# Pools that end with their stage, Toeplitz terms on four row groups, and a new order in the expert stage

## The chip, the cores and the metric

The kernel runs on one core of a Trainium2 chip. The core has five engines that work from queues of their own, each in order: TensorE (PE, with its weight loads listed as PEld), VectorE (DVE), ScalarE (ACT), GpSimd (POOL) and SyncE (SP), which here issues the DMAs. The metric is device microseconds of one execution, the median of several runs. All data are 32-bit floats.

## The reference

Four stages run one after another on x of shape 16 x 256 x 128; each result is added to its input and normalised.

```python
x = ln(x + attn_rel(x))      # 16 heads of 8; logits q.k + q.a_k + k.a_q + a_q.a_k,
                             # a_* = E*[clip(l - m, -64, 64) + 64]; out = attn.v + attn.a_v
x = ln(x + local(x))         # 6 layers: 16 heads of 64, window 32, look-back attention with
                             # rotary terms, then norm, W1 (gelu gate), W2; 64 channels shifted
x = ln(x + causal(x))        # causal attention, 16 heads of 8
x = ln(x + moe(x))           # 8 experts of 64, top 2 of softmax(x @ gate_w)
# moe
gates = softmax(xt @ gate_w);  topk_g, topk_i = top_k(gates, 2)
tok_w = topk_g.sum(-1);        sel = one_hot(topk_i).any(1)
h = gelu(einsum('nd,edh->enh', xt, w1) + b1)
y = einsum('enh,ehd->end', h, w2) + b2
out = einsum('end,ne,n->nd', y, sel, tok_w)
```

## The kernel before

The activations stay in on-chip memory from the first stage to the last, as 16 batches of two tiles of 128 rows (`xb`, and `xa` from the second stage on). PSUM is shared out once for the whole program: `big()` hands out one of 2 buffers of 128 x 1024 (two banks each), `small()` one of 4 buffers of 128 x 512 (one bank each). A stage opens its own pools of on-chip memory when it starts and closes them when it ends; pools lie one behind the other, so the pools of the next stage lie over those of the last. What a new tile waits for is set by the pools that it lies over: all tiles of such a pool must be done with.

Each stage writes out its own order: a list of steps, run again and again for a shifted batch or unit, and at the end `in_order` ties the instructions of each engine to that order. Between stages the planner follows the order of the program, but puts an instruction of a later stage into a hole of an engine when its inputs and its memory are free.

**Relative attention** (`relative_attention`, the first 815 us). One batch is eight turns (`TURNS`), each with one unit of four heads: `weights` (on PE eight transposes at L505 and four matmuls of 32 rows at L517 into a `big`; on DVE four additions with the `rq` terms, L527), `exponentials` (ACT, L543) and `turn_weights` (eight transposes at L562 into two `small`). The terms that depend on position are made once per batch. `diagonal` (128 small matmul passes, L388) makes a skewed copy `spots` of a projection. `chunk` multiplies 32 rows of it by a window of a Toeplitz table, eight matmuls at L413 into one `big`, which lie on two of the four 32-row groups of the array; `rq_chunk` takes them out by two ACT copies (L449), `rk_chunk` by two DVE additions (L470). Four chunks make `rq`, four make `rk`, so a batch has eight. `corners` (L434) makes the far corners. The results go to three sets of tiles, `terms(0..2)`: set 0 for the first half of the rows of every batch, 1 and 2 in turn for the second. All of these, with tables and masks, lie in one pool, `r_one`.

**Local attention and feed-forward** (`local_layers`, 815 to 3741 us). The list `STEPS` runs over 32 tiles of each of 6 layers with up to nine tiles in flight. Its pools (`w_cst`, `a_inp`, `a_one`, `a_two`, `a_thr`, `a_fou`) hold the buffers of the attention and of the feed-forward steps (`f_*`, `a_vo`, `a_g`) together. It begins with `fetch` (the shifted copies `a_xt`, L992 to L994), the weights (L165) and the rotary tables, all issued by SP, then `inputs` (transposes, L1029) and `project` (L1090).

**Causal attention** (`causal_attention`, 3741 to 4115 us) has eight turns per batch again. For batch 0 the steps `join`, `norm`, `scaled`, `turn`, `project_v` and `project` come ahead of the first `weights` (L1534). **Experts** (`experts`, from 4115 us) works on 8 groups of 4 tiles. `turn` makes `xT`, `score` the logits of the gates, `choose` (12 steps on DVE and one on POOL, L1791 to L1808) picks the two best experts of 16 tiles, `first` is the first product with gelu (four matmuls at L1819), `turn_gates` and `weigh` spread the chosen weights over the hidden rows and multiply (L1833, L1835, L1844, L1846), `second` is the second product (L1855, L1862) with the residual addition and the statistics on DVE (L1865 to L1874), `finish` the normalisation on ACT (L1886) and the store.

Of the kernel before, what the change touches and what calls it, by code (L numbers as in the profile page):

```python
# [242 lines left out]
def relative_attention(tc, I, xb, env):  # L243
# [21 lines left out]
    with ExitStack() as ctx:  # L265
        one = ctx.enter_context(tc.tile_pool(name="r_one", bufs=1))
# [6 lines left out]
        def terms(k):  # L273
            rq3[k] = one.tile([P, H, 2, P], F32, name=f"r_rq{k}")
            rk3[k] = one.tile([P, H, P], F32, name=f"r_rk{k}")
            rkc3[k] = one.tile([P, H, P], F32, name=f"r_rkc{k}")

        terms(1)
# [12 lines left out]
        terms(0)  # L291
# [9 lines left out]
        terms(2)  # L301
# [101 lines left out]
        def chunk(table, d, c):  # L403

            ps = big()
            for g in range(4):
                for x in range(2):
                    at = 8 * c + 4 * x + g
                    s_ = at // 16
                    r = rows_of(s_, at // 4 % 4)  # L410
                    o = C0 - 4 * at
                    rows = slice(32 * r, 32 * r + 32)
                    T.matmul(  # L413
                        ps[:, 512 * x + 128 * g : 512 * x + 128 * g + 128],
                        lhsT=table[rows, o : o + P],
                        rhs=d[rows].rearrange("p h t s g i -> p (h t) s g i")[:, :, s_, g, :],
                        start=True,
                        stop=True,
                    )
            return ps  # L420
# [24 lines left out]
        def rq_chunk(b, c):  # L445
            ps = chunk(tq, st[b]["d", "k"], c).rearrange("p (g h t i) -> p t g h i", g=8, t=NT, i=4)
            for t in range(NT):
                o = of(rq3, b, t)[:, :, 0, 32 * c : 32 * c + 32]
                A.copy(o.rearrange("p h (g i) -> p g h i", i=4), ps[:, t])  # L449
# [15 lines left out]
        def rk_chunk(b, c):  # L465
            ps = chunk(tk, st[b]["d", "q"], c).rearrange("p (g h t i) -> p t g h i", g=8, t=NT, i=4)
            pc = pp[:, 32 * c : 32 * c + 32].rearrange("p (g i) -> p g i", i=4).unsqueeze(2)
            for t in range(NT):
                o = of(rk3, b, t)[:, :, 32 * c : 32 * c + 32]
                V.tensor_add(  # L470
                    o.rearrange("p h (g i) -> p g h i", i=4), ps[:, t], bcast(pc, (P, 8, H, 4))
                )
# [186 lines left out]
        def normalise(b, lc):  # L659
# [11 lines left out]
                (1, values, 0),  # L671
                (0, rk_corners, 1),
                (-1, turn),
                (0, rk_chunk, 1),
                (2, turn_weights),
                (0, rk_chunk, 0),
                (0, rk_corners, 0),
                (-1, project),
                (1, exponentials),
                (-1, diagonal, "k"),  # L680
                (0, weights),
            ),
            (
                (2, turn_weights),
# [4 lines left out]
                (0, weights),  # L689
                (1, positions, 1),  # L690
                (2, turn_weights),
                (1, join, 0),
                (1, exponentials),
            ),
            (
                (1, exponentials),
                (0, weights),
                (-1, rq_chunk, 1),
                (1, values, 1),
                (2, turn_weights),  # L700
                (-1, rq_corners, 1),
                (-1, rq_chunk, 2),
            ),
            (
                (1, exponentials),
                (1, join, 1),
                (0, weights),
                (-1, rq_chunk, 0),
                (2, turn_weights),
                (-1, spread_k, 0),  # L710
            ),
            (
                (2, turn_weights),
                (1, exponentials),
                (1, statistics, 1),
                (0, weights),
            ),
            (
                (-1, rq_chunk, 3),
                (0, positions, 0),  # L720
                (1, normalise, 1),
                (-1, rq_corners, 0),
                (1, exponentials),
                (-1, diagonal, "q"),
                (0, weights),
                (-1, rk_chunk, 3),
                (2, turn_weights),
                (0, project_v),
                (1, statistics, 0),
            ),  # L730
            (
                (1, exponentials),
                (2, turn_weights),
                (0, weights),
                (1, normalise, 0),
                (-1, spread_k, 1),
                (-1, rk_chunk, 2),
# [157 lines left out]
def local_layers(tc, I, xa, xb, env):  # L895
# [14 lines left out]
    with ExitStack() as octx:  # L910
# [4 lines left out]
        b2 = cst.tile([P, DEPTH, D], F32, name="w_b2")  # L915
        lng = cst.tile([P, DEPTH], F32, name="w_lng")
        lnb = cst.tile([P, DEPTH], F32, name="w_lnb")
        b1 = cst.tile([P, DEPTH, 2, 3], F32, name="w_b1")
# [31 lines left out]
        fou = octx.enter_context(tc.tile_pool(name="a_fou", bufs=4))  # L950

# [86 lines left out]
        def fold(m):  # L1038
# [7 lines left out]
            if part == 0:  # L1046
# [7 lines left out]
                w["vT"], w["vo"] = wvT, two.tile([P, NP, 2, D], F32, name="a_vo")  # L1054
# [150 lines left out]
        def gather(m):  # L1205
# [16 lines left out]
            g = two.tile([P, H, P], F32, name="a_g")  # L1222
# [13 lines left out]
        def output(m):  # L1236
# [14 lines left out]
            if t == NT - 1:  # L1251
                ffn[i, b] = {"x": shifted(xa[b], fou, "f_xt")}
# [12 lines left out]
        def f_stats(i, g):  # L1265
            f = ffn[i, 2 * g]
            tiles = [ffn[i, 2 * g + k // NT]["x"][:, k % NT, :] for k in range(2 * NT)]
            mv = two.tile([P, 2 * NT, 2], F32, name="f_mv")
            for k, x in enumerate(tiles):
                s6 = two.tile([P, 6], F32, name="f_st")  # L1270
                V.bn_stats(s6, x)
                V.bn_aggr(mv[:, k], s6)
            ve = two.tile([P, 2 * NT], F32, name="f_ve")
# [3 lines left out]
        def f_power(i, g):  # L1277
            f = ffn[i, 2 * g]
            rs = two.tile([P, 2 * NT], F32, name="f_rs")
# [10 lines left out]
        def f_turn(i, g):  # L1290
# [4 lines left out]
            xn = two.tile([P, W], F32, name="f_xn")  # L1295
# [3 lines left out]
        def f_gate(i, g):  # L1299
            f, w = ffn[i, 2 * g], weights[i]  # L1300
            hT = one.tile([P, 3, W], F32, name="f_hT")
# [44 lines left out]
        def f_sum(i, g):  # L1346
# [3 lines left out]
            for k in range(2):  # L1350
                xw = two.tile([P, NT, D], F32, name="f_xw")
# [62 lines left out]
def causal_attention(tc, I, xa, xb, env):  # L1414
# [12 lines left out]
    with ExitStack() as ctx:  # L1427
# [12 lines left out]

        def join(b):
# [26 lines left out]
        def turn(b):  # L1468
            ps = small()
# [6 lines left out]
        def project(b):  # L1476

            ps = small()
# [18 lines left out]
        def project_v(b):  # L1497
            ps = small()
# [200 lines left out]
        for at in range(-NU, N + NU):  # L1699
            for behind, step, *args in TURNS[at % NU]:  # L1700
# [3 lines left out]
                elif 0 <= at // NU - behind < NB:  # L1704
                    step(at // NU - behind, *args)
        env.in_order(first)


def experts(tc, I, xa, out, env):
# [13 lines left out]
    with ExitStack() as ctx:  # L1723
# [3 lines left out]
        glp = ctx.enter_context(tc.tile_pool(name="e_glp", bufs=NH + 1))  # L1727
# [28 lines left out]
        def turn(g):  # L1756
# [4 lines left out]
            if g % 2:  # L1761
# [87 lines left out]
        def second(g):  # L1849
            hT, wT = st[g]["hT"], st[g]["wT"]  # L1850
            po = small()
# [11 lines left out]
            y = two.tile([P, NK, D], F32, name="e_y")  # L1863
            for j in range(2):
                V.tensor_add(  # L1865
                    y[:, NT * j : NT * (j + 1)],
                    po[:, j * S : (j + 1) * S].rearrange("p (t f) -> p t f", t=NT),
                    xa[2 * g + j],
                )
            mv = two.tile([P, NK, 2], F32, name="e_mv")  # L1870
            for k in range(NK):
# [3 lines left out]
            rs = two.tile([P, NK], F32, name="e_rs")  # L1875
            G.tensor_scalar_add(rs, mv[:, :, 1], LN_EPS)
            env.inv_sqrt(rs, rs)
            nm = two.tile([P, NK], F32, name="e_nm")
            G.tensor_mul(nm, mv[:, :, 0], rs)
            G.tensor_scalar_mul(nm, nm, -1.0)  # L1880
            st[g].update(y=y, rs=rs, nm=nm)

# [74 lines left out]
```

## Time and profile before

| what | us |
|---|---|
| median of 3 runs | 4238.94 (4238.55 to 8422.65) |
| the profiled execution | 4239.75 |
| its span, first to last instruction | 4237.9 |
| relative attention, to the last PE instruction | 815.2 |
| local layers, to the last PE instruction of the feed-forward | 3740.7 |
| causal attention, to its last DVE instruction | 4115.7 |
| last instruction of the expert stage | 4237.7 |

The third of the three runs, 8422.65, took twice as long as the other two, which lie 0.4 us apart; the median is one of those two. The page gives busy shares by engine, then the span in 40 slices, the DMA queues, and the chain of work that ended last, followed back from the last instruction. The trace behind it can be asked for one engine's instructions in order of time: such a row has the start, the length of a run of equal instructions, engine and line, tile written and tiles read, shape, count, and in brackets the idle time before it and what ended that. A matmul of 32-bit floats counts twice (two passes), a transpose once.

### The profile page before, as it was taken

The page shows a single profiled execution, that of the slowest core. Times are in us where ns is not written, and L with a number is a line of the kernel's source. Part 1 is how long each engine was busy: PE and PEld are TensorE (multiplying, and loading weights), DVE is VectorE, ACT ScalarE, POOL GpSimd, SP SyncE. Part 2 cuts the span into 40 slices and gives each one's busy share as a digit, 9 for nine tenths or more (in the row PEclk, how much of TensorE's full clock was granted, in tenths as well). Part 3 has the DMA queues.
Part 4 walks back from the last instruction along what each step waited for, and adds up shares of the span by engine and source line. Part 5 has one row for each costly group of instructions (what it writes and reads, how often), then busy time and mean ns, then how long its engine had stood idle before and what let it go on. Part 6 is the DMA issues. An engine that isn't in the chain of part 4 may idle for free.

```text
span 4237.9 us, 149104 instructions
## 1 busy us (share of the span) xinstructions
PE 4110.5 (97%) x62028; PEld 3021.4 (71%) x62028; DVE 3324.1 (78%) x6347; ACT 3301.8 (78%) x11368; POOL 2701.8 (64%) x3176
## 2 busy tenths in 40 slices
PE   8999999899999999999999999999999999989998
PEld 6888888666776677676776777667776677656665
DVE  5655665588888888888888888888888888769974
ACT  3666666578888888888888888888888888869973
POOL 2121211288888888888888888888888888723221
PEclk9999999999999999999999999999999999989999
DMA  1000000110000000000000000000000000000000
GB/s 36 3 3 3 3 3 3 43 30 15 19 20 24 20 21 19 25 18 17 19 20 24 20 20 19 24 18 18 19 15 24 15 14 15 9 2 2 2 8 20
DMA packets 158799, 69.51 MB, mean 16 GB/s; under 512 B 123549, under 2 KB 154276, under 8 KB 158124
## 3 DMA queue, kind: packets, MB, share of 16 engines
q1 hardware_dynamic: 158124, 59.99, 5.6%
q8 instruction: 488, 8.00, 0.8%
q14 instruction: 187, 1.53, 0.1%
HBM read 21.72 MB, written 2.12 MB: 6 GB/s over the span
## 4 chain that ended last, share of the span: by engine, by line
PE 87%; POOL 6%; ACT 3%; issue 2%; DVE 2%; DMA 0%; SPq 0%; POOLq 0%; ACTq 0%; DVEq 0%
PE small L1240 15%; PE big L1090 12%; PE small L1147 8%; PE big L1215 7%; PE big L1162 5%; PE small L1337 3%; PE small L1321 3%; PE big L505 3%; PE small L1578 3%; PE small L562 3%; PE small L1305 3%; PE big L1534 3%; POOL a_u L1129 3%; PE big L517 3%; PE big L413 2%
## 5 line engine op out<-in xcount | busy, mean ns | idle before, releaser
L1183 ACT ACTIVATE a_pr<-a_pr,a_nb 128x64 f32<-128x64 f32 x3072 | 1029.0, 342 | 5.7 <-DVE a_nb L1176 5.7
L1111 POOL TENSOR_TENSOR a_u<-a_u,a_r 128x1024 f32<-128x1024 f32 x384 | 901.2, 2369 | 28.3 <-DVE a_r L1106 23.7
L1129 POOL TENSOR_TENSOR a_u<-a_u,a_y 128x1024 f32<-128x1024 f32 x384 | 722.9, 1904 | 15.1
L1240 PE MATMUL small<-a_vo,a_g 128*128 128x128 f32 x6144 | 717.6, 275 | 1.6 <-ACT a_g L1233 1.6
L1240 PEld LDWEIGHTS small<-a_vo,a_g 128*128 128x128 f32 x6144 | 701.2, 192 | 2.6 <-ACT a_g L1233 2.5
L1101 ACT ACTIVATE a_sq<-big 128x1024 f32<-128x1024 f32 x384 | 392.0, 1022 | 268.9 <-PE big L1090 268.6
L1183 ACT ACTIVATION_READ_ACCUMULATOR a_pr<-a_pr,a_nb 128x1 f32 x3072 | 600.4, 195 | 0.0
L1147 PEld LDWEIGHTS small<-ident,a_u 128*128 128x128 f32 x3072 | 349.5, 141 | 139.9 <-POOL a_u L1129 86.8
L1118 DVE TENSOR_REDUCE a_ss<-a_sq 128x16 f32<-128x1024 f32 x384 | 446.3, 1204 | 0.0
L1147 PE MATMUL small<-ident,a_u 128*128 128x128 f32 x3072 | 401.2, 274 | 23.2 <-POOL a_u L1129 21.1
L1090 PE MATMUL big<-w_k,a_xs 128*128 128x512 f32 x768 | 387.0, 627 | 3.5 <-issue 1.6
L1195 POOL TENSOR_TENSOR a_pr<-a_pr,a_rd 128x1024 f32<-128x1024 f32 x192 | 365.8, 1905 | 13.0 <-DVE a_rd L1194 13.0
L1090 PE MATMUL big<-w_q,a_xs 128*128 128x512 f32 x768 | 362.4, 594 | 0.0
L1162 PEld LDWEIGHTS big<-a_kT,a_qT 64*32 64x32 f32 x24576 | 262.2, 105 | 126.2 <-issue 68.1
L1170 DVE TENSOR_TENSOR a_pr<-big,w_band 128x1024 f32<-128x1024 f32 x192 | 235.2, 1225 | 109.8 <-PE big L1162 109.8
L527 DVE CUSTOM_DVE_ANT_0 r_lg<-big,r_rq 128x256 f32<-128x256 f32 x512 | 186.8, 421 | 155.5 <-PE big L517 67.5
L1102 DVE TENSOR_TENSOR a_u<-big,a_tak 128x1024 f32<-128x1024 f32 x192 | 235.2, 1225 | 90.5 <-ACT a_sq L1101 90.5
L1162 PE MATMUL big<-a_kT,a_qT 64*32 64x64 f32 x24576 | 294.7, 226 | 8.7 <-POOL a_kT L1140 6.2
L1223 ACT COPY a_g<-big 128x1024 f32<-128x1024 f32 x192 | 193.8, 1009 | 105.6 <-PE small L1215 105.1
L1560 ACT ACTIVATE c_lg<-c_lg,c_nb 128x256 f32<-128x256 f32 x512 | 256.8, 520 | 4.7 <-DVE c_nb L1544 4.6
L1090 PEld LDWEIGHTS big<-w_q,a_xs 128*128 128x128 f32 x768 | 143.5, 192 | 164.0 <-issue 128.4
L543 ACT ACTIVATE r_lg<-r_lg,r_nb 128x256 f32<-128x256 f32 x512 | 254.9, 507 | 4.4 <-DVE r_nb L527 4.4
(276 smaller groups left out, 9382.6 us busy)
## 6 DMA issues: line engine op xcount, KB each, us to landing
a_xm<-a_xt SPq DMA_DIRECT2D x96, 96.0 KB
f_xt<-xa SPq DMA_DIRECT2D x96, 64.0 KB
f_xt<-xa SPq DMA_DIRECT2D x96, 63.5 KB
a_xt<-xa SPq DMA_DIRECT2D x80, 64.0 KB
a_xt<-xa SPq DMA_DIRECT2D x80, 63.5 KB
w_k<-in_L_ffn_Wqkv_dram SPq DMA_DIRECT2D x6, 512.0 KB
w_q<-in_L_ffn_Wqkv_dram SPq DMA_DIRECT2D x6, 512.0 KB
w_v<-in_L_ffn_Wqkv_dram SPq DMA_DIRECT2D x6, 512.0 KB
```

The lines of the kernel that those rows point to most:

```text
L1090: T.matmul(ps[:, c * 512 : (c + 1) * 512], lhsT=xs_of[i, b][:, t, 0:P], rhs=weights[i]["qk"[j]][:, c * 512 : (c + 1) * 512], start=True, s ...
L1101: A.activation(sq, ps3, AF.Square)
L1111: G.tensor_add(u, u, r)
L1118: V.tensor_reduce(ss[:, j], st[m]["sq", j], AX.X, ALU.add)
L1129: G.tensor_mul(u, u, bcast(y[:, j].unsqueeze(2), (P, H, DH)))
L1147: T.transpose(ps[:, k, :], u[:, o : o + P], ident)
L1162: T.matmul(ps[q0 : q0 + WIN, e, c, :], lhsT=qT[DH * e : DH * (e + 1), c, q0 : q0 + WIN], rhs=kT[DH * e : DH * (e + 1), c, t * P + q0 : t * ...
L1183: A.activation(s_["pr"][:, h], s_["pr"][:, h], AF.Exp, bias=s_["nb"][:, h : h + 1], accum_out=s_["den"][:, h : h + 1],)
L1195: G.tensor_mul(s_["pr"], s_["pr"], bcast(rd.unsqueeze(2), (P, H, DH)))
L1215: T.matmul(ps[win], lhsT=x[r, t, :], rhs=pT[r, :, o, :], start=(o == 0), stop=(o == 1),)
L1240: T.matmul(ps[:, 0:D], lhsT=st[m]["g"][:, h, :], rhs=weights[i]["vo"][:, h // 2, h % 2, :], start=(h == 0), stop=(h == H - 1),)
L1560: A.activation(lg[:, j], lg[:, j], AF.Exp, bias=nb[:, j : j + 1], scale=-1.0, accum_out=st[b, lc]["den"][:, h : h + 1],)
```

## The change

Four edits are made together.

1. In `relative_attention` the pool `r_one` is split in three. The set `terms(1)`, `spots`, the tables and the projections' weights are in `r_fst`, `terms(0)` is in `r_snd`, the rest is in `r_one`. In `local_layers` the feed-forward buffers, `a_vo`, `a_g` and four small constants go from the front and middle pools to `f_cst`, `f_one`, `f_two` and `f_fou`, which lie behind the pools of the attention.
2. `chunk` becomes `diagonals`: 16 matmuls in a row on all four row groups, into one `big` and two `small`. A batch has four such halves in place of eight chunks. A half is taken out by two operations of 128 x 512 and four of 128 x 256. The eight turns are written anew.
3. In `causal_attention` the turns up to the second unit are given high priority with the planner; the PSUM buffers of `turn`, `project` and `project_v` are a `big` for batch 0.
4. In `experts` both `choose` follow their `score`, ahead of any `first`; `first` runs three groups ahead; `weigh` of the next group stands ahead of `second` of this one; and the last group is closed in two halves, normalised on DVE.

```diff
-        one = ctx.enter_context(tc.tile_pool(name="r_one", bufs=1))
-        terms(1)
+        one = ctx.enter_context(tc.tile_pool(name="r_fst", bufs=1))
+        terms(one, 1)
         spots = one.tile([P, H, NT, 2, 4, 4], F32, name="r_d")
...
-        terms(0)
+        terms(ctx.enter_context(tc.tile_pool(name="r_snd", bufs=1)), 0)
+        one = ctx.enter_context(tc.tile_pool(name="r_one", bufs=1))
...
-        terms(2)
+        terms(one, 2)
...
-        def chunk(table, d, c):
-            ps = big()
+        def diagonals(table, d, s_):
+            both = big()
+            ps = [both[:, 0:512], both[:, 512:1024], small(), small()]
             for g in range(4):
-                for x in range(2):
-                    at = 8 * c + 4 * x + g
-                    s_ = at // 16
-                    r = rows_of(s_, at // 4 % 4)
-                    o = C0 - 4 * at
+                for c in range(4):
+                    r = rows_of(s_, c)
+                    o = C0 - 4 * (16 * s_ + 4 * c + g)
                     rows = slice(32 * r, 32 * r + 32)
                     T.matmul(
-                        ps[:, 512 * x + 128 * g : 512 * x + 128 * g + 128],
+                        ps[c][:, 128 * g : 128 * g + 128],
...
-            return ps
+            for n, p_ in ((8, both), (4, ps[2]), (4, ps[3])):
+                at = 64 * s_ + (0 if n == 8 else 32 if p_ is ps[2] else 48)
+                p_ = p_.rearrange("p (g h t i) -> p t g h i", g=n, t=NT, i=4)
+                for t in range(NT):
+                    yield t, at, n, p_[:, t]
...
+        def rq_half(b, s_):
+            for t, m0, n, p_ in diagonals(tq, st[b]["d", "k"], s_):
+                o = of(rq3, b, t)[:, :, 0, m0 : m0 + 4 * n]
+                A.copy(o.rearrange("p h (g i) -> p g h i", i=4), p_)
...
+            ((0, rk_corners, 0), (0, spread_k, 1), (-1, turn), (2, turn_weights), (-1, project),
+             (0, rk_half, 0), (1, exponentials), (-1, diagonal, "k"), (1, values, 0), (0, weights)),
+            ((1, join, 0), (2, turn_weights), (1, exponentials), (0, weights)),
+            ((1, exponentials), (1, positions, 1), (2, turn_weights), (0, weights)),
+            ((2, turn_weights), (1, exponentials), (0, weights), (-1, rq_corners, 0),
+             (-1, spread_k, 0)),
+            ((1, values, 1), (-1, rq_corners, 1), (1, exponentials), (1, join, 1),
+             (1, statistics, 0), (0, weights), (-1, rq_half, 0), (2, turn_weights)),
+            ((0, weights), (1, statistics, 1), (2, turn_weights), (0, project_v),
+             (1, exponentials), (1, normalise, 1), (-1, rq_half, 1), (-1, diagonal, "q")),
+            ((1, normalise, 0), (2, turn_weights), (0, weights), (1, exponentials)),
+            ((1, exponentials), (0, weights), (-1, rk_half, 1), (2, turn_weights),
+             (-1, rk_corners, 1), (0, positions, 0)),
...
+        cst = octx.enter_context(tc.tile_pool(name="f_cst", bufs=1))
+        fone = octx.enter_context(tc.tile_pool(name="f_one", bufs=1))
+        ftwo = octx.enter_context(tc.tile_pool(name="f_two", bufs=2))
+        ffou = octx.enter_context(tc.tile_pool(name="f_fou", bufs=4))
...
+        def first_of(b):
+            return small() if b else big()
...
+        with tc.high_priority():
+            for at in range(-NU, 2):
+                run(at)
+        for at in range(2, N + NU):
+            run(at)
...
-        choose(0)
-        for g in range(NH):
-            first(g)
+            choose(h)
+        first(0)
+        first(1)
         turn_gates(0)
         weigh(0)
-        choose(1)
+        first(2)
+        turn_gates(1)
         for g in range(NG):
-            if g + 1 < NG:
-                turn_gates(g + 1)
-            if g + NH < NG:
-                first(g + NH)
-            second(g)
+            if g + 3 < NG:
+                first(g + 3)
             if g + 1 < NG:
                 weigh(g + 1)
+            second(g)
+            if g + 2 < NG:
+                turn_gates(g + 2)
             if g:
                 finish(g - 1)
-        finish(NG - 1)
...
+        def close(g, j):
+            y = two.tile([P, NT, D], F32, name="e_yh")
+            added(y, g, j)
+            mv, rs = moments(y)
+            for t in range(NT):
+                V.tensor_scalar(
+                    y[:, t], y[:, t], mv[:, t, 0:1], rs[:, t : t + 1], ALU.subtract, ALU.mult
+                )
+            store(g, j, y)
```

Here the new `TURNS` is set with several steps to a line. `close` is called inside `second` after the second and the fourth tile of the last group; `moments`, `added` and `store` are the bodies of the old `second` and `finish`, and `measure` keeps the statistics of the other groups. `e_glp` has 4 buffers in place of 5, and `xT` of groups 5 and 7 is copied by ACT in place of DVE. `rk_half` is `rq_half` with the table `tk` and the DVE addition of `pp`.

## The prediction

> **What bounds the kernel now.** I read the page first, for the engine that ends last.
>
> ```profile
> PE 4110.5 (97%) x62028; PEld 3021.4 (71%) x62028; DVE 3324.1 (78%) x6347; ACT 3301.8 (78%) x11368; POOL 2701.8 (64%) x3176
> ...
> PE 87%; POOL 6%; ACT 3%; issue 2%; DVE 2%; DMA 0%; SPq 0%; POOLq 0%; ACTq 0%; DVEq 0%
> ```
>
> PE is the bound, so a part of the change pays if it shortens PE's work or closes a hole in it. The busy time by stretches shows where holes are: one batch of the first stage, then the three stretches in which stages change or end.
>
> ```profile
> 339.20:387.60 48.40, 47.36 (x1061) 41.24 (x1053) 29.18 (x101) 29.73 (x93) 9.79 (x16) 1.00 0.01 3
> 815.20:904.00 88.80, 66.31 (x800) 41.34 (x800) 59.67 (x65) 51.22 (x171) 64.34 (x72) 0.83 0.30 76
> 3681.00:3760.00 79.00, 58.05 (x480) 39.21 (x468) 32.27 (x88) 34.67 (x114) 21.28 (x30) 0.88 0.02 5
> 4113.00:4238.00 125.00, 101.54 (x578) 74.76 (x578) 54.18 (x131) 43.73 (x79) 24.67 (x39) 0.88 0.08 23
> ```
>
> Columns: length, PE, PEld, DVE, ACT, POOL busy, then granted clock. The batch has 1 us of hole in 48.4; the others have 22, 21 and 23, at a clock of 0.83 to 0.88. Between them lie some 2800 us that the change leaves as they are: only addresses move there.
>
> What a chunk costs, from the chain of waits in order of time, in the first stage:
>
> ```profile
> 743.51 0.62 PE big L434 x32
> 744.14 1.09 PE big L413 x16
> ...
> 746.52 0.33 PE big L517
> 747.64 1.90 PE small L562 x16
> ...
> 757.56 1.06 PE big L517 x8
> 758.62 0.89 PE big L413 x16
> ```
>
> Three prices for the same work: 1.09 alone; 0.89 behind a `weights` on the same row groups; and next to nothing at 746.52, where L517 and the chunk after it run side by side on different groups: 1.12 in all, 0.06 more than L517 alone. The order by hand already uses four row groups there. That is the trap here: halving the matmuls' time doesn't halve the path.
>
> The stage changes, on PE and POOL:
>
> ```profile
> 814.92 0.27 PE L642 MATMUL small<-ident,r_oT 128*128 128x128 f32 x1
> 821.62 0.66 PE L1029 MATMUL small<-ident,a_xt 128*128 128x128 f32 x2 [6.43 <-DMA a_xt<-xb]
> 823.79 3.75 PE L1090 MATMUL big<-w_k,a_xs 128*128 128x512 f32 x4 [1.51 <-DMA w_k<-in_L_ffn_Wqkv_dram]
> ```
>
> ```profile
> 3741.78 0.72 POOL L1443 TENSOR_TENSOR c_y<-xb,xa 128x256 f32<-128x256 f32 x1 [13.45 <-issue]
> ```
>
> ```profile
> 4159.40 0.75 DVE L1865 TENSOR_TENSOR e_y<-small,xa 128x256 f32<-128x256 f32 x2
> ```
>
> ```profile
> 4191.24 2.26 PE L1855 MATMUL small<-e_w,e_hT 128*128 128x128 f32 x8 [2.13 <-DVE e_hT L1846]
> 4201.53 2.35 PE L1855 MATMUL small<-e_w,e_hT 128*128 128x128 f32 x8 [2.04 <-DVE e_hT L1846]
> ```
>
> SP issues the first load of the local layers at 815.27, just when the last reader of `r_one` ends (815.19). `join` of batch 0 (3741.78) waits for the last feed-forward addition (3741.56), though its input is long done: memory, not data. In the expert stage the last groups come every 10.3 us with 2 us of hole, and the eight passes after it take 2.3 in place of 1.06: the halved clock follows the hole.
>
> **The change part by part.** All sums are against the profiled execution, 4239.75 (span 4237.9), 0.8 above the median.
>
> *Halves for chunks.* In the batch from 711.8 to 759.5 the chain has three chunks at 1.09, one at 0.89 and four hidden at 0.06: 3 x 1.09 + 0.89 + 4 x 0.06 = 4.40. A half gives each of four groups the four matmuls that a chunk gives two, so at full rate it lasts as long as one chunk. Two halves stand behind full-array matmuls (`project`, `project_v`): 1.09 each. Two stand behind `weights`; two of their groups are taken by L517 first, so they end 0.89 after it, however the other two run: 2 x 1.09 + 2 x 0.89 = 3.96. Gain 0.44 x 16 = 7.0. No row shows four groups all with 128-column passes. The nearest, the 1.12 block, has 24 passes, 47 ns each; were that a floor, 32 passes take 1.49 and not 0.85, each half 0.64 more: 4 x 0.64 x 16 = 41 lost, net +34. At the other end, all halves at 0.89: 3.56, a gain of 13. I take full rate, since 47 ns is set there by L517's longer passes.
>
> The skill's page "TensorE: Matmul & The Clock Gate", LDWEIGHTS, has the load grow with columns and not with rows, about 107 ns for 128; my estimate from it is 3.4 us for 32 loads in series, 4 x 3.4 = 13.7 per batch against 4.40, and so a part that loses 149 us where the rows give a gain of 7. The row with 47 ns per pass shows that loads of different row groups do overlap.
>
> Taking out: a chunk had two ACT copies of 0.589 (L449) or DVE additions of 0.683 (L470). A half has two of these and four of 128 x 256, priced by L1473 (0.373) and L1865 (0.416): 2.67 on ACT against 2.36 for two chunks, 3.03 on DVE against 2.73. Per batch 0.6 more on each, hidden by 19 us of idle in 48.4; uncovered it costs 19 us in all. But a half holds two of four `small` meanwhile. Next behind `rq_half` come `turn_weights` (1.9) on the other two, `weights` (2.08), and then `turn_weights` needs the first two: 4.0 us of cover against 2.67 and whatever ACT is late. Thin; between 0 and 2.67 per half I take 0.05, nearest to the first, as the batch shows almost no hole today with two `big` in the same play: 64 x 0.05 = 3. Stage: -4.
>
> At its end the chain spends 767.5 to 772.2 on DVE (`rk_corners`, `rk_chunk`); `values` (1.88 + 1.09) now stands between `rk_half` and `weights`: -2 (0 to -4.6).
>
> *Pools, first to second stage.* By tile sizes `r_fst` holds 46.8 KB and `r_snd` 32.8 KB; weights, `xa`, constants and `a_xt` need 52 KB and lie over these two alone, free after batch 15's first half, near 790. SP then loads during the last 25 us; nothing else queues on it. PE starts L1029 at 815.3 and L1090 near 816.3, not 823.8 (-7.5), at full clock (3.6 for eight passes, not 6.5). Late next: the five table operations on POOL (826.33 to 828.31), which wait for `a_two`, over `r_one`, and mix with the last statistics (to 820.1); done near 820, so DVE's first L1102 comes at 820 and not 828.7. I take -8.5 (-6 to -10.3).
>
> *Second to third stage.* `c_*` now lies over attention pools only, last read by PE at 3711.9. From there to 3759.7 PE has 3.6 (L1240) + 16.9 (two feed-forward groups at the lengths from 3717 to 3726) + 6.2 (the first causal steps, at the lengths that they have from 3770 on) = 26.7 us of full-clock work in 47.8: at most 21 to gain. The feed-forward's chain lasts to 3740.7; batch 0's ten turns cost PE some 4.7 inside it, then a third `weights` and a `turn` (1.5): 3744.5 in place of 3759.7. I take -15. If the planner puts batch 0's steps in front as a block, their chain (3741.78 to 3752.64, 10.9) delays the feed-forward: -8. Two table switches (1.28 each) may come if an exponential falls among the gelus; ACT has the holes.
>
> *Experts.* PE from 4129.9 to 4228.7 (98.8) holds, at the prices of the unthrottled group at 4169.8 to 4179.4, 32 x 0.86 (L1819) + 8 x (0.49 + 1.07 + 4.56) (L1833, L1844, `second`) = 76 of work; 22 is hole and slow clock. `choose(1)` no longer stands between `weigh(0)` and the additions (4150.2 to 4159.5), and `weigh` ahead of `second` takes the statistics (2.6) out of the loop. New: `score(1)`'s two DVE steps queue behind `choose(0)`, whose last step moves to about 4132.8, so the exponential and the first gelu come 2.9 later; `weigh(0)`, (6) and (7) wait for the copy at L1835, 0.6 and its semaphores. Waste left 8: -15. Closing by halves: from the last matmul to ACT's end 6.3; now 0.4 + 0.9 on DVE, 0.2 + 0.7 on POOL, 0.6 on DVE and hand-overs, 3.2: -3. Together -18 (-12 to -23).
>
> Sum: -4 - 2 - 8.5 - 15 - 18 = -47.5; 4238.94 - 47.5 = 4191.
>
> **Rivals.** *Slower: the `small` pool.* Two smalls held for the whole taking-out, with PE waiting it out behind each half: 64 x 2.7 = 173, less 50 gained: +122, 4361. It decides from 0.8 us per half (50/64). For it: 4.0 us of cover is thin; against it: ACT and DVE are busy 60%. "TensorEngine Tiling (Array Packing)", PSUM Bottleneck, warns of just this, that after a speedup by four the copies may bound; by it alone the sum would be this rival's.
>
> *Four groups not at full rate:* stage +34 + 3 in place of -4: 4232.
>
> *The pools don't part*, because one early tile reaches over `r_one`, or the planner sets batch 0 in a block: -8.5 and -7 are lost, 4207.
>
> *Everything at its good end:* -13 - 4.6 - 10.3 - 21 - 23 = -72: 4167. Even that is 1.7%, under the 2% that a measurement here tells from no change (85 us, 4154).
>
> **Numbers.** Forecast 0.66; pools 0.12; four groups 0.08; good end 0.10; slower rival 0.04, in part over 2%. Range 4166 to 4218: it takes in the good end and the pools, and leaves out the two bad ones. Faster by 2%: 0.03, same 0.94, slower 0.03.
>
> **What would show it.** L413's successor: 32 passes in 1.1, nothing waiting on `small`; a batch of 47.4 to 48.0. L1029 within 1 us of 815 less the stage's gain, no DMA ending its wait. L1443 right after the last gather, L1534 among the feed-forward's matmuls, clock 1.0 there. In the expert stage groups every 7 us at the end and no half clock. A batch over 48.4, or a hole behind a half that ACT or DVE ends, would prove me wrong; so would SP's first load still at the end of the stage.

## The result and the profile after

The changed kernel takes 4179.53 us (median of 4 runs, 4176.58 to 4185.57), the one before beside it 4242.03 (median of 4 runs, one of which took 8422.65 while the others took 4238.55 to 4245.13): without that run a ratio of 0.9857, 95% interval [0.9838, 0.9877]. It is 1.4% faster: the interval is clear of 1, but the change stays under the 2% from which it would count as faster here. The profiled execution is the slowest of the four: 4185.57, span 4183.8, that is 54.2 below the 4239.75 of before. The page, then the busy time in the stretches that answer to those of before (a batch of the first stage, and the three stretches in which stages change or end):

```profile
PE 4081.6 (98%) x62028; PEld 2993.4 (72%) x62028; DVE 3326.7 (80%) x6413; ACT 3300.4 (79%) x11432; POOL 2702.0 (65%) x3176
...
PE 87%; POOL 6%; ACT 3%; issue 2%; DVE 1%; DMA 0%; SPq 0%; POOLq 0%; DVEq 0%; ACTq 0%
```

```profile
233.20:280.20 47.00, 46.40 (x970) 39.94 (x973) 26.23 (x98) 29.66 (x97) 9.17 (x16) 0.96 0.01 3
806.00:895.00 89.00, 73.86 (x997) 49.56 (x998) 68.63 (x74) 61.21 (x213) 74.69 (x83) 0.88 0.13 25
3658.00:3723.00 65.00, 52.13 (x425) 34.45 (x421) 29.61 (x87) 36.32 (x113) 21.04 (x30) 0.92 0.02 5
4075.00:4184.00 109.00, 95.51 (x578) 69.88 (x578) 54.89 (x134) 40.89 (x77) 24.86 (x39) 0.92 0.09 26
```

PE still ends the chain, with 29 us less busy time for the same 62028 instructions. The first stretch after the first stage is as long as before (89 us) and holds 74 us of PE work in place of 66. Holes of 15 us in all are left there, and of 13 in each of the other two.

The half of the terms, from the chain of waits in order of time: once alone, once behind `weights`.

```profile
599.41 0.31 PE big L415 x2
...
600.51 1.92 PE big L389 x128
...
606.42 1.06 PE big L521 x8
607.48 0.06 PE big L415 x2
...
608.33 0.05 PE small L415 x2
608.38 1.02 PE small L566 x8
```

Alone, the 32 passes take 599.41 to 600.51, 1.10; behind L521, the successor of L517, they end 0.90 after it (607.48 to 608.38). The stage changes, on PE and POOL:

```profile
805.95 0.27 PE L646 MATMUL small<-ident,r_oT 128*128 128x128 f32 x1
806.06 0.38 PE L1034 MATMUL small<-ident,a_xt 128*128 128x128 f32 x2
807.02 1.98 PE L1095 MATMUL big<-w_k,a_xs 128*128 128x512 f32 x4 [0.58 <-ACT a_xs L1035]
808.85 1.88 PE L1095 MATMUL big<-w_q,a_xs 128*128 128x512 f32 x4
```

```profile
3690.30 0.73 POOL L1452 TENSOR_TENSOR c_y<-xb,xa 128x256 f32<-128x256 f32 x1 [2.10 <-PE small L1220]
```

```profile
3699.74 1.99 PE L1543 MATMUL big<-c_ks,c_q 32*128 32x512 f32 x8 [0.48 <-POOL c_ks L1501]
...
3713.56 0.30 PE L1299 MATMUL small<-ident,f_xt 128*128 128x128 f32 x1 [2.20 <-issue]
...
3715.90 5.49 PE L1310 MATMUL small<-f_xn,w 128*128 128x512 f32 x6 [0.87 <-ACT f_xn L1301]
3721.18 3.21 PE L1326 MATMUL small<-f_xn,w 128*128 128x512 f32 x6
```

No transfer ends a wait at the first change any more. At the second, batch 0's sum on POOL (L1452, L1443 before) stands right behind the local attention's last products (L1220), 51 us earlier than before, and its third-stage `weights` (L1543) fall among the feed-forward's matmuls. But a hole of 2.20 in the last feed-forward group has stayed, and the matmuls behind it run at half the clock: six passes of L1310 in 5.49, at a granted clock of 0.50 from 3715.90 to 3721.20. The expert stage, its start and its last groups:

```profile
4080.03 6.53 PE L1788 MATMUL small<-e_gw,e_xT 128*128 128x8 f32 x32 [2.56 <-DMA e_gw<-in_L_ffn_gate_w_dram]
...
4158.67 1.14 PE L1860 MATMUL big<-e_wT,e_esel 32*128 32x512 f32 x8 [0.73 <-ACT e_wT L1851]
...
4165.64 1.14 PE L1860 MATMUL big<-e_wT,e_esel 32*128 32x512 f32 x8 [0.73 <-ACT e_wT L1851]
4166.71 1.16 PE L1872 MATMUL small<-e_w,e_hT 128*128 128x128 f32 x8
```

The last groups come 6.97 apart, with 0.73 of wait and the eight passes at full clock (1.16). What is left lies at the start: a wait of 2.56 for a load and slow passes behind it (granted clock 0.54 from 4080.00 to 4086.50).

Against before, landmark by landmark in the two profiled executions, the 54 us are: first stage 9.0; first to second stage 11.9; 2.3 drift in the second stage; second to third 14.5; experts 16.4. The forecast had 6, 8.5, 0, 15 and 18.

### The profile page after: what moved, and what is told of

It reads as the page before. It is cut to its first block, busy times and chain, and to the rows that moved or that the text cites. A ratio compares the mean times of both kernels' runs of the same rounds, so it can differ in the third digit from the quotient of the medians.

```text
span 4183.8 us, 149153 instructions
## 1 busy us (share of the span) xinstructions
PE 4081.6 (98%) x62028; PEld 2993.4 (72%) x62028; DVE 3326.7 (80%) x6413; ACT 3300.4 (79%) x11432; POOL 2702.0 (65%) x3176
## 4 chain that ended last, share of the span: by engine, by line
PE 87%; POOL 6%; ACT 3%; issue 2%; DVE 1%; DMA 0%; SPq 0%; POOLq 0%; DVEq 0%; ACTq 0%
PE small L1245 15%; PE big L1095 12%; PE small L1152 8%; PE big L1220 7%; PE big L1167 5%; PE small L1342 3%; PE big L521 3%; PE small L1326 3%; PE small L566 3%; PE small L1310 3%; POOL a_u L1134 3%; PE small L1587 3%; PE big L1543 3%; PE big L509 3%; PE small L1220 2%
## 5 line engine op out<-in xcount | busy, mean ns | idle before, releaser
L1188 ACT ACTIVATION_READ_ACCUMULATOR a_pr<-a_pr,a_nb 128x1 f32 x3072 | 588.8, 192 | 0.0
```

What stands on the lines that cost most here:

```text
L1188: A.activation(s_["pr"][:, h], s_["pr"][:, h], AF.Exp, bias=s_["nb"][:, h : h + 1], accum_out=s_["den"][:, h : h + 1],)
```

## The experiments

All start from the changed kernel. Each ratio is to the kernel before, run beside it. Stages are compared with the changed kernel's profile, from landmark to landmark, since a whole time moves by 3 to 14 us from run to run of one kernel. A landmark is read in one profile, so it has a spread too. Where the code of a stretch is the same, the first stage ends between 800.2 and 808.6 (ten profiles); from nine tenths into the second stage to the middle of the third takes from 3.0 less to 1.9 more than in the changed kernel (ten); from the first score to the last second matmul takes from 1.3 less to 2.4 more (seven). A difference inside these bounds is not shown.

**The third stage without high priority.**

```diff
-        with tc.high_priority():
-            for at in range(-NU, 2):
-                run(at)
-        for at in range(2, N + NU):
-            run(at)
+        for at in range(-NU, N + NU):
+            run(at)
```

> The changed kernel without the high priority of the first ten causal turns; nothing else differs. Theory A (memory placement carries the gain: once the causal pools lie over attention pools alone, the planner puts batch 0's steps into the holes of the feed-forward's end by itself): within 4 us of the changed kernel (4176 to 4184), the first causal weights matmul on PE still ahead of the last feed-forward matmul. Rival B (the priority is what gets them in): these steps run behind the feed-forward's end, some 12 us later, 4190 to 4194.

4184.47, 0.9881 [0.9868, 0.9895]. The third stage's first `weights` (3714.24) still come ahead of the last feed-forward matmul (3717.40), as Theory A has it. Measured from nine tenths into the second stage, that matmul comes 7.0 us earlier than in the changed kernel, the first `weights` 17.5 later, and the boundary is 4.3 us longer in all, somewhat more than its spread: batch 0 delays the feed-forward less, and less of it is hidden there.

**One pool for the first stage's buffers,** as before the change.

```diff
-        one = ctx.enter_context(tc.tile_pool(name="r_fst", bufs=1))
+        one = ctx.enter_context(tc.tile_pool(name="r_one", bufs=1))
...
-        terms(ctx.enter_context(tc.tile_pool(name="r_snd", bufs=1)), 0)
-        one = ctx.enter_context(tc.tile_pool(name="r_one", bufs=1))
+        terms(one, 0)
```

> The changed kernel with the first stage's tiles in one pool again (r_fst and r_snd joined to r_one). Theory A (what a first load waits for is the whole pool that it lies over): SP's first load of the local layers comes again at the last PE instruction of the first stage (about 806), PE idles some 6 us there, total +9 to +12: 4188 to 4192. Rival B (the loads were hidden anyway, the table operations on POOL and the latency of the fill decide): under +3.

4189.19, 0.9886 [0.987, 0.9901]. In its SP queue the first input load stands right behind the stage's end (801.47) again; on PE the wait and the halved clock are back:

```profile
801.54 0.70 SPq L996 DMA_DIRECT2D a_xt<-xb  x1
```

```profile
808.45 0.66 PE L1033 MATMUL small<-ident,a_xt 128*128 128x128 f32 x2 [6.99 <-DMA a_xt<-xb]
810.08 3.75 PE L1094 MATMUL big<-w_k,a_xs 128*128 128x512 f32 x4 [0.96 <-DMA w_k<-in_L_ffn_Wqkv_dram]
```

A tenth into the second stage it is 11.8 us behind the changed kernel, measured from the first stage's end. So without the parted pools all of the 11.9 that the change gained there is lost. They don't earn it alone: a later run, with the feed-forward's buffers back in their old pools, loses 3.8 at the same place.

**Old chunks and old turns,** with the pools of the change: `chunk`, `rq_chunk`, `rk_chunk` and the first stage's `TURNS` of before.

```diff
-        def diagonals(table, d, s_):
+        def chunk(table, d, c):
...
-                (0, rk_half, 0),
+                (0, rk_chunk, 0),
```

> The changed kernel with the chunks, rq_chunk, rk_chunk and the turns of before in the first stage; the pools stay split. Theory A (halves gain 0.44 per batch on the path and the rest of the stage's 9 us comes from the turns): last PE instruction of the stage 7 to 10 us later than in the changed kernel, 4186 to 4190, a batch of 48.0. Rival B (the halves themselves give nothing, the earlier first batch gives all 6): +5 to +6 and a batch of 47.2 as with halves. Rival C (the two small buffers held cost something): less than +4.

4197.2, 0.9911 [0.9897, 0.9924]. The stage's end is that of before (815.23; 815.19), 9.0 behind the changed kernel's and inside Theory A's 7 to 10, and a batch takes 47.8. So the terms and their turns carry the whole of the first stage's gain; they were undone together, and this run doesn't part the one from the other. The time is over Theory A's 4186 to 4190: the profiled execution (4195.52) lies 10.0 above the changed kernel's, which was the slowest of its four, and the median 17.7 above.

**The expert stage of before.**

```diff
-            if g + 1 < NG:
-                weigh(g + 1)
             second(g)
...
+            if g + 1 < NG:
+                weigh(g + 1)
```

The whole function is that of before: `choose`, `first`, `turn_gates` and the closing too.

> The changed kernel with the expert stage of before, whole. Theory A (the parts add up): the stage takes 122 us again in place of 106, total +16 to +20: 4195 to 4199, with groups every 10.3 us at the end and the half clock after each hole. Rival B (the stage's gain came in part from an earlier or warmer start): less than +13.

4198.58, 0.9915 [0.9902, 0.9928]. From the first score to the last second matmul 18.3 us longer, with the closing 20.6. In the profile of before, the same stage is 4.1 shorter than here; part of that is clock, which from the first score to the first second matmul was granted at 0.85 there and at 0.77 here.

**The diagonals, one row group after the other.**

```diff
-            for g in range(4):
-                for c in range(4):
+            for c in range(4):
+                for g in range(4):
```

> The sixteen diagonal matmuls of a half in another order: all four of a row group in a row, then the next row group, instead of the row groups by turns. Same matmuls, same sums. Theory A (row groups work side by side only when neighbours in the instruction stream lie in different row groups, so the order by turns is what makes a half cost about 1 us): each half takes 2.5 to 4 us instead of 1.1, and with 64 halves that is 90 to 190 us more: 4270 to 4370. Rival B (the engine takes matmuls of free row groups past waiting ones anyway): a half stays within 0.3 us of 1.1 and the time within 10 us of the changed kernel's (4170 to 4190). Rival C (the halves' cost is hidden behind other work of the first stage): halves long, time within 10 us.

4273.03, 1.0075 [1.006, 1.009]: 0.75% slower than before the change. Its chain of waits, at a half that stands alone:

```profile
560.75 1.30 PE big L415 x13
562.38 1.11 PE small L415 x13
563.49 1.92 PE big L389 x128
```

The same 16 matmuls (32 passes) take 560.75 to 563.49, 2.74 in place of 1.10: 86 ns a pass against 34. Batches last 52.1 and the stage ends 83 us later. Theory A held, at the low end of its 90 to 190 us (93.5 between the medians): a half costs 1.6 more alone and less where neighbours overlap it. The order of two loops is worth 83 us of the stage. It changes more than the row group, though: each of the four `ps[c]` lies in a PSUM bank of its own, so neighbours by turns also write to different banks, and in turn to the same one. No run parts the two causes.

The Trainium skill, "TensorE: Matmul & The Clock Gate", puts the sustained rate of pairs of a load and a 128-column matmul at some 81 ns per matmul (section "Back-to-back issue gap"), and says in its section on row groups (Part 3) that a load overlaps with matmuls in flight only where the row group differs. The 86 ns in turn lie near the first, and the 34 ns by turns fit the second. The estimate of 107 ns per load in series, which the prediction took from the same page, was not reached even in turn.

**The small buffers taken out first.**

```diff
-            for n, p_ in ((8, both), (4, ps[2]), (4, ps[3])):
+            for n, p_ in ((4, ps[2]), (4, ps[3]), (8, both)):
```

> The two small buffers of each half are taken out before the big one instead of after it. Theory A (no one waits for a small buffer, as the changed kernel's trace shows: 3 us of such waits in the whole stage): first stage's end within 2 us of its spread in the other runs (800 to 806), time 4174 to 4186. Rival B (the forecast's term of 3 us for stalls on small buffers is paid, hidden in waits that the trace puts down to others): 3 to 6 us faster, 4172 or less.

4189.92, 0.9878 [0.9861, 0.9894]. Neither: the first `weights` come 3.9 us later, the stage's end 7.3 later (813.5, outside the spread). PE at the corners of batch 0, this kernel and then the changed one:

```profile
48.59 0.69 PE L440 MATMUL big<-r_d,r_tkc 32*64 32x64 f32 x32 [2.20 <-DVE r_rk L474]
```

```profile
47.01 0.69 PE L440 MATMUL big<-r_d,r_tkc 32*64 32x64 f32 x32 [0.83 <-DVE r_rk L474]
```

What PE waits for is the `big` buffer, not the small ones. Where no other work fills in, at the stage's head, it now waits 1.4 longer, and the next half runs at half the clock (granted 0.50 from 51.00 to 54.50; 1.00 in the changed kernel from 47.70 to 54.00). So a stall on the taking out exists, but on the other kind of buffer and at the head: from batch 1 to batch 15 a batch takes 47.4 in either order.

**The feed-forward's buffers and four constants back among the attention's,** with the high priority kept.

```diff
-        cst = octx.enter_context(tc.tile_pool(name="f_cst", bufs=1))
...
-        fone = octx.enter_context(tc.tile_pool(name="f_one", bufs=1))
-        ftwo = octx.enter_context(tc.tile_pool(name="f_two", bufs=2))
-        ffou = octx.enter_context(tc.tile_pool(name="f_fou", bufs=4))
+        fone, ftwo, ffou = one, two, fou
```

> The feed-forward's buffers and constants go back into the attention's pools, as before the change; the turns and the high priority stay. Theory A (the memory placement carries about 10 of the 14.5 us that the change gained from second to third stage, the priority the rest): the third stage's weights load only when the feed-forward has ended, first c weights 8 to 14 us later against the stage before it, time +8 to +15 us: 4188 to 4195. Rival B (the order of the turns is what counts): within 3 us, 4177 to 4183. Rival C (pools of different size also shift the second stage): a difference that grows inside the second stage.

4202.71, 0.9908 [0.9893, 0.9923]: more than expected. Second to third stage is 15.6 us longer, and first to second 3.8. There the copy L1032 into `a_xs` ends a wait of 4.35 before the first projection; the copy itself starts at 812.76, behind L665, the last normalisation of the first stage, whose result it doesn't read, while its input was ready at 808.8. That is a wait for memory too. POOL, then PE, at the second change:

```profile
3726.03 0.72 POOL L1449 TENSOR_TENSOR c_y<-xb,xa 128x256 f32<-128x256 f32 x1 [13.27 <-issue]
```

```profile
3722.45 2.50 PE L1339 MATMUL small<-w,f_hT 85*128 85x128 f32 x20 [0.37 <-DVE f_hT L1331]
...
3736.88 5.81 PE L1540 MATMUL big<-c_ks,c_q 32*128 32x512 f32 x12 [2.90 <-POOL c_ks L1498]
```

Batch 0's sum waits for the end of the feed-forward again, in spite of its priority, and its `weights` come 12 us after it. The priority is worth some 4 where memory is free. Where it isn't, no gain shows: the mixed pools lose 15.6 with it, and the kernel before, which lacks it, 14.5.

**`weigh` behind `second` again** in the experts' loop.

```diff
-            if g + 1 < NG:
-                weigh(g + 1)
             second(g)
+            if g + 1 < NG:
+                weigh(g + 1)
```

> In the experts' loop the weighing of the next group goes back behind the second matmul of this one; the gates' turn stays one group ahead. Theory A (weighing ahead is what takes the wait of 3 us out of each of the last groups): the last groups stand 9.5 to 10.5 us apart again instead of 7.0, the last second matmul 9 to 14 us later against the score's start, time 4189 to 4194. Rival B (turning the gates a group ahead is what counts): groups stay at 7 to 7.5 us, time within 3 us, 4177 to 4183.

4194.48, 0.9889 [0.9875, 0.9904]. PE in two of the last groups:

```profile
4155.76 0.68 PE L1872 MATMUL small<-e_w,e_hT 128*128 128x128 f32 x4 [2.13 <-DVE e_hT L1862]
...
4166.21 0.83 PE L1872 MATMUL small<-e_w,e_hT 128*128 128x128 f32 x4 [2.04 <-DVE e_hT L1862]
```

They are 10.45 apart again; from the first second matmul to the last it takes 74.4 in place of 62.0 (the same in every profile with the changed loop), 12.4 us longer, all of it in the latter half of the loop. Theory A held: this one line is most of the experts' gain.

**Both choices behind both scores; the gates' weights loaded early; the gates' turn two ahead and four turns of high priority.** Three kernels, each with the edits of the one before it. The load goes into a buffer of the pool of `xa`, issued before the third stage.

```diff
-            choose(h)
+        choose(0)
+        choose(1)
```

> Both choices are set behind the second score, so that VectorE takes the second score's maximum before the first choice. Theory A (the first gelu comes late because the second score's two VectorE steps queue behind the choice, as the forecast's term for the experts' stage says, 2.9 us): first gelu 2.5 to 3.5 us earlier after the score's start, but the first gates come up to 2 us later, net -3 to 0 us at the last second matmul, time 4176 to 4180. Rival B (the gates' turn ends last, not the gelus): +1 to +3 us.

4183.4, 0.9868 [0.9851, 0.9884]. From the first score to the last second matmul 2.6 us longer: rival B, if narrowly. Some 0.8 of it may be clock: three other profiles with the changed expert stage are 0.8 longer as well, at a granted 0.76 from the first score to the first second matmul (0.77 here, 0.80 in the changed kernel). The first gelu starts 2.7 behind the start of the scores' last pass in place of 5.3, but the first gates come later too, and PE now waits for those (0.36 before their turn, none in the changed kernel).

```diff
+        env.gw = xap.tile([P, NE], F32, name="e_gw")
...
+        nc.sync.dma_start(env.gw, I["L1_ffn_gate_w"])
         causal_attention(tc, I, xa, xb, env)
...
-        gw = cst.tile([P, NE], F32, name="e_gw")
-        nc.sync.dma_start(gw, I["L1_ffn_gate_w"])
+        gw = env.gw
```

> As both_scores, and the gate's weights are loaded before the third stage, into a buffer that lies free from the second stage on. Theory A (the wait of 2.56 us at the first score is for this load, and the halved clock of the scores behind it follows the hole): no wait there, first score 2.5 us earlier, its 32 matmuls in 3 to 4 us instead of 6.5, so 5 to 6 us less than both_scores alone: 4170 to 4175. Rival B (the wait is also one for the turned inputs, 1.3 us of VectorE and ScalarE copies behind the turns): 1 to 2 us earlier and the clock still halved, 4174 to 4179.

4177.69, 0.9854 [0.9838, 0.987]. PE at the scores:

```profile
4071.28 3.74 PE L1789 MATMUL small<-e_gw,e_xT 128*128 128x8 f32 x32 [1.29 <-ACT e_xT L1781]
4074.88 3.29 PE L1776 MATMUL small<-ident,xa 128*128 128x128 f32 x16
...
4091.91 0.63 PE L1850 MATMUL small<-ident,e_wide 128*128 128x128 f32 x4 [1.30 <-DVE e_wide L1825]
```

The wait falls from 2.56 to 1.29 and doesn't vanish: the turned inputs end it now, as rival B has it. The 32 passes fall from 6.53 to 3.74, as Theory A has it, but the passes behind them are at half clock (granted 0.54 from 4075.00 to 4078.50). From the third stage's last matmul to the last second matmul it is 5.0 us less than in the kernel with both choices last, which is Theory A's size, and the later gates (1.30 of wait) take part of that back: 2.6 net against the changed kernel, hardly more than the spread. The time is in rival B's range, over Theory A's 4170 to 4175.

```diff
-            for at in range(-NU, 2):
+            for at in range(-NU, 4):
...
-            wT = two.tile([P, W], F32, name="e_wT")
+            wT = thr.tile([P, W], F32, name="e_wT")
...
+        first(2)
         turn_gates(0)
         weigh(0)
-        first(2)
         turn_gates(1)
         for g in range(NG):
+            if g + 2 < NG:
+                turn_gates(g + 2)
...
             second(g)
-            if g + 2 < NG:
-                turn_gates(g + 2)
```

> As early_gates, and: the third group's first matmuls ahead of the first gates' turn; the gates' turn two groups ahead, with a third buffer; the high priority reaches four turns of the third stage instead of two. Theory A (the holes of 0.7 us before the last groups and of 2.2 us in the last feed-forward group can be filled with work that is ready): the last groups without the wait of 0.73, 1.4 us; the hole at the feed-forward's end filled, 2 to 5 us less up to a steady third stage: 4164 to 4171. Rival B (the planner sets the two more turns ahead of the feed-forward, whose chain then ends later, and exponentials fall between gelus with a change of table each): second to third stage 0 to 5 us longer, 4170 to 4178.

4178.07, 0.9854 [0.9839, 0.9869]. The waits of 0.73 before the last groups are gone (2.0 us in the third quarter of the loop). The two more turns of priority bring nothing that shows: second to third stage is 2.7 us shorter than in the changed kernel's profile, and 3.0 in the kernel with both choices last, which has the old priority. The hole in the feed-forward's last group is 1.92 in place of 2.20, and the time stays above Theory A's 4164 to 4171.

**Early load and gates two ahead alone,** the choices where the change has them.

> The changed kernel with two things added: the gate's weights loaded ahead of the third stage, and the gates' turn two groups ahead with a third buffer; the choices stay where the change has them, each behind its own score. Theory A (both holes are on the path, and the choice between the scores is the better place, as both_scores showed): from the third stage's last matmul to the last second matmul 6 to 9 us less than in the changed kernel (101 us there), time 4170 to 4175. Rival B (what the load gains is lost again, since the second score's VectorE steps still queue behind the first choice, which ends at its own time): 2 to 4 us less, time 4175 to 4178.

4179.09, 0.9853 [0.9839, 0.9867]. From the third stage's last matmul to the last second matmul 5.6 us less: between the two theories; the second score's steps still queue behind the first choice (1.06 of wait for the first gelu). In the whole time that can't be told from the changed kernel's 0.9857; none of these versions is shown to beat it.

## Why the prediction was right, and by which terms

The forecast, 4191, held: measured 4179.5, in its range. Its 47.5 us fell short by 7 in the profiled executions and by 12 against the median from which it counted (4238.94).

**Halves at full rate: right.** 1.10 alone and 0.90 behind `weights` were the 1.09 and 0.89 of the sum. From the first `weights` of batch 1 to those of batch 15, a batch takes 47.0 to 47.5 in the ten profiles whose first stage is that of the change (mean 47.3), 47.8 before and with the old chunks and turns: 0.47 a batch where the sum had 0.44. How much of it is the new turns is not shown. The loops' order decides the rate, and four groups that don't run side by side have their price: 4273.

**Three us of stalls on the small buffers: wrong.** From 40 us on, PE's waits ahead of a matmul into a `small` that another engine ends come to 3.1 us in the whole stage, 2.22 of them in one wait at 787.57, and none is ended by the taking out of a half (L454, L474). What can be late is the `big`.

**The first stage's end: wrong, small.** From the last batch's first `weights` to the last `join` it is 42.8 us before and 43.2 after (43.1 to 44.8 in the ten): the 2 us of gain didn't come.

**What the first stage's sum left out is its head.** The first `weights` of batch 1 start at 103.1 before, at 94.8 to 99.7 in the ten profiles (99.3 in the changed kernel's), and at 101.8 with the old chunks. At the head no other work hides a chunk, so the prices of the steady batch (0.06 for four of eight) don't hold there. The chain of waits of the kernel before, at that place:

```profile
48.01 1.30 DVE r_rk L470 x2
49.31 0.14 issue
49.44 0.69 PE big L434 x32
50.14 0.38 PE small L316 x2
50.52 0.12 issue
50.64 3.38 PE big L413 x32
54.01 1.06 PE big L434 x32
```

Chunk, additions and corners follow one another, and the last two chunks take 3.38, at about half the clock (granted 0.57 from 50.70 to 54.00). The head gives 3.4 to 8.3 us, of which 1.3 came with the old chunks too. So the first stage's term of 4 was mis-sized: 6.6 for fourteen batches (0.47 each) and about 4 for the head (the mean of the ten, 5.3, less 1.3), with no stalls against them. That the stage came to 9.0 for 6 is in part luck: the head was left out, while the stalls and the end were terms that didn't come, one charged and one credited.

**First to second stage: right mechanism, low in size.** Without the parted pools 11.8 are lost; the sum had 8.5 and an end of 10.3. Of these 7.8 are the wait up to the first projection (8.87 behind the last `join` before, 1.07 after), as forecast; its next eight passes at half the clock (6.47 to 3.70) were counted in part.

**Second to third: 14.5 for 15.** Memory, not data, was the cause, as the sum said: with the pools mixed all of it goes. Its picture was too bright in one point: the clock is not 1.0 there but 0.92 (3658 to 3723).

**Experts: 16.4 for 18.** `weigh` ahead of `second` carries 12.4, the closing by halves 2.3 (3 forecast). The 2.9 that the sum charged for the second score behind the first choice is there (the first gelu at 4099.01, 5.3 after the start of the scores' last pass, and 2.7 with both choices last), but taking it away made nothing faster: two chains end there nearly together, the gelu's and the gates'. The waste left at the start, 8 in the sum, is the 2.56 of load and slow passes, and not all of these come from the load: the clock falls a second time behind the scores, where PE didn't wait (last section).

Left open: the drift of 2.3 us in the second stage, which the change leaves as it is; and why the same first stage ends between 800.2 and 808.6 in ten profiles. Holes of 0.2 to 1.9 us that the trace calls issue, many of them within runs of 32 to 128 small matmuls, come and go there; whether they make the difference was not shown:

```profile
571.01 0.96 PE small L618 x33
571.97 0.53 issue
572.50 1.08 PE small L618 x31
```

## What to carry to other kernels

A stage that waits for its predecessor's last instruction may wait for memory alone: ask which tiles lie over which, and give buffers that end early, or that end late, a pool of their own; priority in the planner helps only after that. Matmuls that use a part of the rows ran side by side here when neighbours in the stream lay on different row groups (and wrote to different PSUM banks), so the order of two loops can be worth more than the change around it. And price the head and the end of a stage by themselves: what a steady batch hides is paid in full there.

## What the runs showed of the hardware

- 32 passes of 32 rows by 128 columns: 1.10 us over four row groups by turns, 2.74 with the same passes group after group.
- A wait of PE of 2 us and more was followed by half the clock in several places: 2.20 before L1299 (then six passes of L1310 in 5.49), 2.56 before L1788 (32 passes in 6.53), 2.04 to 2.63 in the experts' old order. But not always: in the changed kernel 2.22 before L566 (787.57) was followed by a granted 1.00 up to 794.40, and in the kernel before 2.31 before L1215 (3700.70) by 1.00 up to 3704.10. The Trainium skill's page "TensorE: Matmul & The Clock Gate", in its part on the clock gate, gives one idle window of about 3.4 us as the condition; in the first of these rows shorter waits were enough, and the rows decide.
- The clock also fell with no wait ahead of it, behind the scores' passes, which move only 8 columns each. In the kernel before, PE was busy without a gap from 4126.70 to 4130.10, nearly all of it with these passes, at a granted 1.00, and the next 3.40 us were granted 0.50. With the gates' weights loaded early the 32 passes took 3.74, from 4071.30 to 4075.00 at 1.00, and the 16 transposes behind them 3.29 against 1.91 at full clock. Why, no run shows.
